# Stacked q and k loaded in two halves of groups, and the first maxima begun with the even groups

## The chip, the cores and the metric

One core of a Trainium2 chip runs the whole program. The metric is the device time of one execution in microseconds, median of several. Engines named below: PE is TensorE, DVE is VectorE, ACT is ScalarE, POOL is GpSimd, SP is SyncE, which here only issues transfers.

## The reference, cut to what matters

The kernel computes one transformer layer for 32 sequences of 256 tokens of width 128 in float32.

```python
Q, K, V = (split_heads(x @ W.T + b) for W, b in ((Wq, bq), (Wk, bk), (Wv, bv)))  # 16 heads of 8
scores = Q @ K.T / sqrt(8)                     # 256 x 256 for each head
scores = where(j > i, -inf, scores) - (i - j)  # causal, with a linear decay
x = layernorm(x + softmax(scores) @ V @ Wo.T + bo)
h = silu((x @ w1.T) * s1) * ((x @ w2.T) * s2)  # 128 -> 512
h = gelu((h @ h1.T) * sh1); h = gelu((h @ h2.T) * sh2)
x = layernorm(x + (h @ w3.T) * s3)
```

## The kernel before

The 32 sequences are worked in 16 **pairs** of two sequences, 512 tokens each. The 16 heads of a pair lie in 8 **groups** g of two heads, one head on partitions 0 to 63, the other on 64 to 127.

**Projection** (`project`, L314). x is transposed on PE (pxT), copied by DVE (xT), multiplied with wq_sb and wk_sb (pq, pk). `halves` (L295) splits each product in two parts that matmuls take without loss: ACT writes the high part (qhi, khi), DVE the rest (qlo, klo). Partition p*64 + d*8 + g of these tiles holds element d of head p of group g; the order comes from the way in which ACT copies the loaded weights to wq_sb and wk_sb (L165).

**Stacks** (`stack`, L305). For the scores, each group needs its own matrix with the elements of the head under each other: rows for the high and the low parts, mixed with constant rows for mask and decay that `fill` (L185) writes once into the buffers qs and ks (two each, used by pairs in turn). `stack` brings the parts there by transfers within the on-chip memory: four for q, four for k, of 0.25 MB each, all 8 groups in each. The first two pairs are stacked by SP (q) and ACT (k), pair 2 likewise at the end of step 0, all later ones by SP alone.

Every engine works through its instructions in the order in which they are written here; ACT's transfers stand among its arithmetic. Each transfer of SP and ACT takes one of eight completion semaphores in turn, and in the compiled order waits until the last transfer on that semaphore has landed.

**Maxima** (`row_maxima`, L373). A pair has 12 tiles of scores, numbered 3a, 3a+1, 3a+2 for a = 0 to 3: tile 3a holds the later half of the tokens of group 2a, tile 3a+1 that of group 2a+1, tile 3a+2 the earlier half of both groups. Each is eight or four matmuls and four mask matmuls on PE (s), and one DVE reduction (m) over 128x1024 numbers. Three buffers (ps_s) hold such tiles. `maxima_to_rows` (L407) transposes the maxima (pm), splits them (mhi on ACT, mlo on DVE) and brings them into qs by small transfers.

**Weighing** (`weigh`, L430) computes the scores again, now with the maxima as a row, takes exp on ACT (e) and masks on POOL. `outputs` (L470) multiplies with the values (pa), copies the result on ACT (oT), turns it back (pt) and divides (rec, on); `finish` (L512) multiplies with Wo (pon, onT, po) and adds x. The values of a pair come from `project_values` (L339): pv on PE, vaug on DVE.

**Order.** The start (L684 to L720) is written out by hand: project, fill and stack pairs 0 and 1, values of pair 0, maxima of pair 0 (tiles 0 to 5), values of pair 1, rows of groups 0 to 3, loads of the layer weights, tiles 6 to 11, rows of groups 4 to 7, two tiles of pair 1. Then `step(n)` (L725) weighs pair n, takes the maxima of pair n+1, projects and stacks pair n+2, and runs the feed-forward part (`feed`) of pair n-1. Step 0 has no feed-forward part; it checks the layer weights instead. In step 0 the stack of pair 2 is issued after the last weighing and before the last oT.

```python
    stack(1, "q", sp)
    stack(1, "k", act)
    project_values(0)
...
    for i in range(6):
        row_maxima(0, i)
    project_values(1)
    maxima_to_rows(0, (0,))
    loaded = load_layers(once)
    for i in range(6, 3 * G):
        row_maxima(0, i)
```

Of the kernel before, what the change touches and what calls it, by code (L numbers as in the profile page):

```python
# [8 lines left out]
F32 = mybir.dt.float32  # L9
# [3 lines left out]
AF = mybir.ActivationFunctionType  # L13
ALU = mybir.AluOpType
# [5 lines left out]
H, HD = 16, 8  # L20
# [9 lines left out]
W = 8  # L30
PAIRING, ROWS1, ROWS2 = 2, 62, 64


G, C = 4, 4
# [27 lines left out]
def tile_attn_ffn(  # L62
# [24 lines left out]
    pe, vec, act, sp = (InOrder(tc, e) for e in (nc.tensor, nc.vector, nc.scalar, nc.sync))  # L87
# [44 lines left out]
    nothing = const.tile([P, 1], F32, name="nothing")  # L132


    wq_sb = const.tile([P, D], F32, name="wq_sb")
    wk_sb = const.tile([P, D], F32, name="wk_sb")
    bq_sb = const.tile([P, 1], F32, name="bq_sb")
    bk_sb = const.tile([P, 1], F32, name="bk_sb")
# [4 lines left out]

    tri_q = const.tile([P, P], BF16, name="tri_q")
    raws = []
    for src, w_bias, bias, nm, eng in (
        (wqT, bq_sb, bq, "q", act), (wkT, bk_sb, bk, "k", sp),
    ):
        raw = setup.tile([P, D], F32, name=f"raw{nm}")
        eng.dma_start(out=raw, in_=src)  # L150
        raws.append(raw)
        for p in range(2):

            eng.dma_start(
                out=w_bias[64 * p : 64 * p + 64, :],
                in_=bias.rearrange("(f p) d e -> p d e f", p=2)[p],
            )

    def prepare(func):

# [2 lines left out]
    prepare(AF.Identity)  # L163
    act.dma_start(out=wv_sb, in_=wvT)
    for raw, dst, scale in zip(raws, (wq_sb, wk_sb), (HD**-0.5, 1.0)):  # L165
        act.activation(
            dst.rearrange("i (p d g) -> i p d g", p=2, g=W),
            raw.rearrange("i (g p d) -> i p d g", p=2, g=W), AF.Copy, scale=scale,
        )
    act.activation(bq_sb, bq_sb, AF.Copy, scale=HD**-0.5)  # L170
    act.dma_start(out=bv_sb, in_=bv.to_broadcast([P, D]))
    act.dma_start(out=bo_sb, in_=bo.to_broadcast([P, D]))

# [4 lines left out]
    def constants(nm, col):  # L178
        t = setup.tile([P, TOK], F32, name=f"{nm}const")
        vec.tensor_scalar(t, number, col["lo"], col["value"], ALU.is_ge, ALU.mult)  # L180
        vec.scalar_tensor_tensor(t, number, col["hi"], t, ALU.is_le, ALU.mult)
        vec.scalar_tensor_tensor(t, number, col["slope"], t, ALU.mult, ALU.add)
        fills[nm] = t, col["base"]

    def fill(dst, nm, eng, groups=slice(0, W)):  # L185
        t, base = fills[nm]
        to = dst[:, groups, :]
        t = t.unsqueeze(1).to_broadcast([P, groups.stop - groups.start, TOK])
        if eng is act:
            act.activation(to, t, AF.Identity, bias=base)  # L190
        else:
            eng.tensor_scalar(to, t, base, None, ALU.add)

    def column(nm):
        return setup.tile([P, 1], F32, name=f"col_{nm}")

    q, k = (
        {w: column(f"{nm}_{w}") for w in ("lo", "hi", "value", "slope", "base")} for nm in "qk"
    )
# [3 lines left out]
    for col, at in ((k, 64), (q, 0)):  # L203
# [6 lines left out]
    k["slope"] = q["base"]  # L210
    constants("k", k)
    fill(ks[0], "k", act)

    make_identity(nc, ident_b)
    nc.gpsimd.memset(tri_q, 0.0)
# [2 lines left out]
        out=tri_q, in_=tri_q, pattern=[[-1, P]], base=0, channel_multiplier=1,  # L218
# [30 lines left out]
    def load_layers(pool):  # L249
        got = {}  # L250
        for nm, src, k, o in layers:
            got[nm] = pool.tile([P, k, o], F32, name=f"{nm}_sb")
            sp.dma_start(out=got[nm], in_=src.rearrange("(k p) o -> p k o", p=P))
        return got
# [31 lines left out]
    def work(nm):  # L286
        return ps_w.tile([P, 512], F32, name=nm, tag="work")

    def two(nm):
        return ps_s.tile([P, 2, 512], F32, name=nm, tag="s")  # L290

    pairs = {}


    def halves(n, ps, bias, nm):  # L295
        pool = setup if n == 1 else hlp
        hi = pool.tile([P, TOK], F32R, name=f"{nm}hi_{n}", tag=f"{nm}hi")
        act.activation(hi, ps, AF.Identity, bias=bias)
        lo = pool.tile([P, TOK], F32R, name=f"{nm}lo_{n}", tag=f"{nm}lo")
        vec.scalar_tensor_tensor(  # L300
            lo, ps, bias, hi.bitcast(F32), ALU.add, ALU.subtract
        )
        return hi, lo

    def stack(n, nm, eng=sp):  # L305
        for r, part in {
            "q": ((0, 0), (1, 0), (2, 1), (3, 1)), "k": ((0, 0), (2, 0), (1, 1), (3, 1))
        }[nm]:
            eng.dma_start(
                out=pairs[n][nm][PAIRING + r :: W, :, :].bitcast(F32),  # L310
                in_=pairs[n][nm + "s"][part].bitcast(F32),
            )

    def project(n):  # L314
        xn = xs[n]
# [23 lines left out]
    def project_values(n):  # L339
        xT, v = pairs[n]["xT"], vaug[n % 2]  # L340
        pairs[n]["v"] = v
        pv = work(f"pv_{n}")
        for t in range(NT):
            pe.matmul(
                pv[:, t * D : (t + 1) * D], lhsT=xT[:, t * P : (t + 1) * P], rhs=wv_sb,
                start=True, stop=True,
            )
        to = v[:, :, 0 : H // 2 * VSLOT].rearrange("p t (r c k) -> p t r c k", r=2, c=C)
        src = pv.rearrange("p (t r e c d) -> p t r e c d", t=NT, r=2, e=2, c=C)
        bias = bv_sb.rearrange("p (r e c d) -> p r e c d", r=2, e=2, c=C)  # L350
        for r in range(2):
            for e in range(2):
                vec.tensor_tensor(
                    to[:, :, r, :, 2 * e * VHEAD : 2 * e * VHEAD + HD], src[:, :, r, e],
                    bias[:, r, e].unsqueeze(1).to_broadcast([P, NT, C, HD]), ALU.add,
                )
# [3 lines left out]
    def mask(blocks):  # L360


        for p, f in ((0, 0), (1, 1), (0, 1), (1, 0)):
            s, first, count = blocks(p)
            rows = slice(64 * p, 64 * p + 64)
            pe.matmul(
                s[64 * f : 64 * f + 64, :, first + 64 * f : first + 64 * f + 64],
                lhsT=ident_b[rows, rows],
                rhs=tri_q[rows, rows].unsqueeze(1).to_broadcast([64, count, 64]),
                start=False, stop=True, tile_position=(64 * p, 64 * f),  # L370
            )

    def row_maxima(n, i):  # L373

        q, k, m = (pairs[n][w] for w in "qkm")
        mv = m.rearrange("i b c (e p g) -> i e p g b c", e=2, p=2)[:, i // 6]
        a, part = divmod(i, 3)
        if part < 2:
            g = 2 * a + part
            s = two(f"s1_{n}_{g}").rearrange("i p (b j) -> i p b j", b=2)  # L380
            for b in range(2):
                for p in range(2):
                    rows = slice(64 * p, 64 * p + ROWS1)
                    pe.matmul(
                        s[:, p, b, :], lhsT=q[rows, g, b * T + P : (b + 1) * T],
                        rhs=k[rows, g, b * T : (b + 1) * T], start=(b == 0), stop=False,
                    )
            mask(lambda p: (s[:, p], P, 2))
            vec.tensor_reduce(mv[:, :, g % C, :, 1], s, AX.X, ALU.max, negate=True)
            return  # L390
        s = two(f"s1_{n}_{a}d").rearrange("i p (h b j) -> i p h b j", h=2, b=2)
        for h in range(2):
            for b in range(2):
                for p in range(2):
                    rows = slice(64 * p, 64 * p + ROWS1)
                    i0 = b * T
                    pe.matmul(
                        s[:, p, h, b, :], lhsT=q[rows, 2 * a + h, i0 : i0 + P],
                        rhs=k[rows, 2 * a + h, i0 : i0 + P],
                        start=(h == 0 and b == 0), stop=False,  # L400
                    )
        mask(lambda p: (s[:, p].rearrange("i h b j -> i (h b) j"), 0, 4))
        vec.tensor_reduce(
            mv[:, :, 2 * a % C : 2 * a % C + 2, :, 0], s, AX.X, ALU.max, negate=True
        )
# [273 lines left out]
    def run(gen):  # L679
        for _ in gen:  # L680
            pass
# [5 lines left out]
    fill(qs[0], "q", vec)  # L687
    run(ahead)
    stack(0, "q", sp)
    stack(0, "k", act)  # L690
    fill(ks[1], "k", act)
    ahead = project(1)
    next(ahead)
    fill(qs[1], "q", vec)
    run(ahead)
    stack(1, "q", sp)
    stack(1, "k", act)
    project_values(0)
    for a in range(G):
        act.dma_start(  # L700
            out=wo_sb[C * HD * a : C * HD * (a + 1), :],
            in_=woT[:, :, a, :].rearrange("c d o -> (c d) o"),
# [4 lines left out]
    yp = enter(tc.tile_pool(name="yp", bufs=2))  # L707
    lctx = ctx.enter_context(ExitStack())
    once = lctx.enter_context(tc.tile_pool(name="once", bufs=1))
    for i in range(6):  # L710
        row_maxima(0, i)
    project_values(1)
    maxima_to_rows(0, (0,))
    loaded = load_layers(once)
    for i in range(6, 3 * G):
        row_maxima(0, i)
    maxima_to_rows(0, (1,))
    load_scales()
# [165 lines left out]
```

## Time and profile before

| what | value |
|---|---|
| median of 3 runs | 822.67 us (822.67 to 824.28) |
| the profiled execution | 824.84 us |
| its span, first to last instruction | 822.9 us |
| mean granted clock of PE | 0.968 |
| PE busy in the span | 781.9 us (95%) |
| DVE busy | 635.9 us (77%) |
| ACT busy | 527.7 us (64%) |
| POOL busy | 260.6 us (32%) |
| stack transfers | 116 of 0.25 MB |

The page shows averages over the whole span. The start is short and differs from the rest, so it is read from the timeline. A line of the timeline has the start in us from the span's start, the length in us, the engine, the line (L58 is the helper that records most operations), the operation, the tile written and the tiles read, the shape, and how many instructions are merged; in brackets stands how long the engine had been idle before and who ended that. A q behind an engine's name marks its queue: an issue of a transfer, not work of the engine. Stretches give the busy time of each engine in a window, the clock that PE was granted (1.00 is full) and what the DMA engines moved.

### The profile page before, as it was taken

The numbers are of one execution on the slowest core, as the hardware profiler recorded it, in microseconds if no ns is written. First come the engines' busy times: TensorE is split into PE (matmuls) and PEld (weight loads), VectorE is DVE, ScalarE is ACT, GpSimd is POOL, SyncE is SP. The second block draws the span as 40 slices with busy tenths as digits, with TensorE's granted clock in tenths as the row PEclk, the third lists the DMA queues.
The fourth block names the chain that finished last, engine by engine and source line by source line (L and its number), as shares of the span: only waits on it lengthen the run. The fifth ranks groups of instructions, "written<-read, shape, count | busy, mean of one in ns | idle before, by whom it ended". The sixth has DMA issues, their size and how long they took to land.

```text
span 822.9 us, 17420 instructions
## 1 busy us (share of the span) xinstructions
PE 781.9 (95%) x7046; PEld 554.9 (67%) x7046; DVE 635.9 (77%) x1247; ACT 527.7 (64%) x719; POOL 260.6 (32%) x341
## 2 busy tenths in 40 slices
PE   4897999999999999999999999999999999999995
PEld 1664576676767677676767767676766767666673
DVE  6786777878788887888878887888888788873674
ACT  5055556667676776666576676657666676758673
POOL 5032413323142332414242341424233232424211
PEclk8569999999999999999999999999999999999997
DMA  6824040402304040320404041140404023000001
GB/s 148 209 63 108 14 106 14 105 16 60 73 14 106 27 107 14 81 53 14 106 27 106 14 104 29 36 97 15 107 26 104 4 57 64 14 5 14 0 3 41
DMA packets 39898, 47.49 MB, mean 58 GB/s; under 512 B 3968, under 2 KB 21632, under 8 KB 39808
## 3 DMA queue, kind: packets, MB, share of 16 engines
q1 hardware_dynamic: 37152, 42.82, 21.8%
q10 hardware_dynamic: 2656, 3.48, 1.9%
q8 instruction: 57, 0.93, 0.5%
q14 instruction: 33, 0.27, 0.1%
HBM read 7.48 MB, written 4.19 MB: 14 GB/s over the span
## 4 chain that ended last, share of the span: by engine, by line
PE 80%; ACT 5%; DVE 3%; issue 1%; DMA 1%; SPq 0%; POOL 0%; ACTq 0%; POOLq 0%; DVEq 0%
PE peven L58 14%; PE podd L58 14%; PE pa L58 11%; PE pw L58 10%; PE s L58 10%; PE s_2d L58 2%; PE s_3d L58 2%; PE s_1d L58 2%; PE po L58 2%; ACT e L58 2%; PE pt L58 2%; PE pk L58 2%; PE pv L58 2%; PE s_0d L58 1%; PE pq L58 1%; ACT yT L58 1%
## 5 line engine op out<-in xcount | busy, mean ns | idle before, releaser
L58 DVE TENSOR_REDUCE m<-s 128x4 f32<-128x1024 f32 x128 | 155.6, 1218 | 11.0 <-PE s L58 9.4
L58 ACT ACTIVATE e<-s 128x1024 f32<-128x1024 f32 x128 | 130.6, 1021 | 44.9 <-PE s L58 30.6
L463 POOL TENSOR_SCALAR_AFFINE_SELECT e<-e 128x512 f32<-128x512 f32 x128 | 83.1, 650 | 221.5 <-ACT e L58 192.2
L58 PE MATMUL podd<-h,h_near 128*128 128x512 f32 x512 | 131.4, 403 | 0.9 <-DVE m L58 0.5
L58 PE MATMUL peven<-hodd,h_near 128*128 128x512 f32 x512 | 122.7, 396 | 0.0
L58 PEld LDWEIGHTS peven<-hodd,h_near 128*128 128x128 f32 x512 | 95.7, 187 | 23.4 <-DVE hodd L58 0.3
L58 PEld LDWEIGHTS podd<-h,h_near 128*128 128x128 f32 x512 | 91.7, 188 | 23.1 <-DVE h L58 3.5
L58 ACT ACTIVATE hodd<-podd,sh 128x512 fp32r<-128x512 f32 x64 | 44.1, 688 | 62.8 <-PE podd L58 62.6
L58 PE MATMUL pw<-x1T,w_near 128*128 128x512 f32 x256 | 75.6, 418 | 1.1 <-DVE h0w L58 1.1
L58 PEld LDWEIGHTS s<-qs,ks 64*128 64x128 f32 x512 | 39.1, 189 | 51.9 <-DVE m L58 17.9
L58 PE MATMUL pa<-e,vaug 128*32 128x256 f32 x1024 | 72.2, 397 | 0.0
L274 POOL TENSOR_TENSOR rsa<-rsa,half 128x4 f32<-128x4 f32 x16 | 16.3, 1018 | 175.9 <-DVE rsa L58 175.9
L58 DVE SCALAR_TENSOR_TENSOR h0w<-pw,s,sg 128x512 f32<-128x512 f32 x64 | 47.9, 748 | 30.3 <-ACT sg L58 30.3
L58 PE MATMUL s<-qs,ks 64*128 64x256 f32 x512 | 65.6, 336 | 1.0 <-ACT e L58 0.5
L58 DVE TENSOR_TENSOR heven<-evenw,heven 128x512 fp32r<-128x512 f32 x64 | 44.2, 692 | 26.6 <-ACT evenw L58 26.1
L58 ACT ACT_TABLE_LOAD x47 | 60.3, 1283 | 3.5 <-issue 2.6
L58 ACT ACTIVATE sg<-pw,s 128x512 f32<-128x512 f32 x64 | 43.7, 684 | 28.2 <-PE pw L58 27.8
L58 ACT ACTIVATE heven<-peven,sh 128x512 fp32r<-128x512 f32 x48 | 33.4, 696 | 39.8 <-PE peven L58 39.8
L58 PE MATMUL s<-ks,qs 62*128 62x256 f32 x512 | 55.8, 297 | 2.6 <-ACT e_0d L58 2.1
L58 PEld LDWEIGHTS pw<-x1T,w_near 128*128 128x128 f32 x256 | 43.4, 188 | 18.4 <-ACT nothing L58 5.8
L581 POOL TENSOR_TENSOR h<-h0w,h 128x512 fp32r<-128x512 f32 x31 | 40.0, 1291 | 43.5 <-DVE h L58 41.2
L58 DVE TENSOR_TENSOR hodd<-oddw,hodd 128x512 fp32r<-128x512 f32 x64 | 43.7, 684 | 10.0 <-ACT oddw L58 9.8
(147 smaller groups left out, 1415.7 us busy)
## 6 DMA issues: line engine op xcount, KB each, us to landing
qs<-qhi SPq DMA_DIRECT2D x32, 256.0 KB
qs<-qlo SPq DMA_DIRECT2D x32, 256.0 KB
ks<-khi SPq DMA_DIRECT2D x26, 256.0 KB
ks<-klo SPq DMA_DIRECT2D x26, 256.0 KB
x<-in_x_dram SPq DMA_DIRECT2D x16, 256.0 KB
out_dram<-z SPq DMA_DIRECT2D x15, 256.0 KB
ks<-khi ACTq DMA_DIRECT2D x6, 256.0 KB
ks<-klo ACTq DMA_DIRECT2D x6, 256.0 KB
```

The source lines that it names most:

```text
L58: return lambda *args, **kw: self.tc.keep_in_program_order(call(*args, **kw))
L274: nc.gpsimd.tensor_tensor(rs, rs, half[:, 0:NT], ALU.pow)
L463: nc.gpsimd.affine_select(out=on_diagonal, in_=on_diagonal, pattern=[[0, on_diagonal.shape[1]], [1, P]], base=0, channel_multiplier=-1, co ...
L581: (nc.gpsimd if o < (1 if final else 2) else vec).tensor_tensor(h[:, 1, o, :], whole, h[:, 0, o, :].bitcast(F32), ALU.subtract)
```

## The change

Four things are changed.

- The columns of wq_sb and wk_sb are reordered so that the even groups lie on partitions 0 to 63 of the projected tiles and the odd groups on 64 to 127. ACT copies each weight in two instructions instead of one. The biases then are one run of memory each: SP loads both with one transfer each, where ACT and SP had issued two each. The scaling of bq_sb moves behind the first fill of ks.
- `stack` issues eight transfers of half the size instead of four: first the four for the even groups, then the four for the odd groups. This holds for all 16 pairs.
- For pair 1 alone, the DVE instructions that write qlo and klo are put off (`due`) until two maxima of pair 0 have been taken (`run_due`).
- The tiles of pair 0 are taken in the order 0, 3 (before the stack of pair 1), then 6, 9, 1, 2, 4, 5, then the values of pairs 0 and 1 and the rows of the first half, then 7, 8, 10, 11.

```diff
+    for w_bias, bias in ((bq_sb, bq), (bk_sb, bk)):
+        sp.dma_start(out=w_bias, in_=bias.rearrange("c d (e o) -> (c d e) o", o=1))
...
-        act.activation(
-            dst.rearrange("i (p d g) -> i p d g", p=2, g=W),
-            raw.rearrange("i (g p d) -> i p d g", p=2, g=W), AF.Copy, scale=scale,
-        )
-    act.activation(bq_sb, bq_sb, AF.Copy, scale=HD**-0.5)
+        for f in range(2):
+            act.activation(
+                dst[:, 64 * f : 64 * f + 64].rearrange("i (p d e) -> i p d e", p=2, e=C),
+                raw.rearrange("i (e f p d) -> i f p d e", f=2, p=2, e=C)[:, f], AF.Copy,
+                scale=scale,
+            )
...
     fill(ks[0], "k", act)
+    act.activation(bq_sb, bq_sb, AF.Copy, scale=HD**-0.5)
...
-        vec.scalar_tensor_tensor(
-            lo, ps, bias, hi.bitcast(F32), ALU.add, ALU.subtract
+        due.append(
+            lambda: vec.scalar_tensor_tensor(lo, ps, bias, hi.bitcast(F32), ALU.add, ALU.subtract)
         )
+        if n != 1:
+            run_due()
         return hi, lo
...
+        for f in range(2):
+            for r, part in {
+                "q": ((0, 0), (1, 0), (2, 1), (3, 1)), "k": ((0, 0), (2, 0), (1, 1), (3, 1))
+            }[nm]:
+                eng.dma_start(
+                    out=pairs[n][nm][PAIRING + r :: W, f::2, :].bitcast(F32),
+                    in_=pairs[n][nm + "s"][part][64 * f : 64 * f + 64, :].bitcast(F32),
+                )
...
     run(ahead)
+    for i in (0, 3):
+        row_maxima(0, i)
+    run_due()
     stack(1, "q", sp)
     stack(1, "k", act)
-    project_values(0)
...
-    for i in range(6):
+    for i in (6, 9, 1, 2, 4, 5):
         row_maxima(0, i)
+    project_values(0)
     project_values(1)
...
-    for i in range(6, 3 * G):
+    for i in (7, 8, 10, 11):
         row_maxima(0, i)
```

More of the change, by code (lines that the diff above doesn't have):

```diff
@@ L145, in tile_attn_ffn @@
     raws = []
-    for src, w_bias, bias, nm, eng in (
-        (wqT, bq_sb, bq, "q", act), (wkT, bk_sb, bk, "k", sp),
-    ):
+    for src, nm, eng in ((wqT, "q", act), (wkT, "k", sp)):
         raw = setup.tile([P, D], F32, name=f"raw{nm}")
@@ L151, in tile_attn_ffn @@
         raws.append(raw)
[L152 to L156, printed above, removed]
-            )
+    for w_bias, bias in ((bq_sb, bq), (bk_sb, bk)):
+        sp.dma_start(out=w_bias, in_=bias.rearrange("c d (e o) -> (c d e) o", o=1))
     def prepare(func):
@@ L165, in tile_attn_ffn @@
     for raw, dst, scale in zip(raws, (wq_sb, wk_sb), (HD**-0.5, 1.0)):
-        act.activation(
-            dst.rearrange("i (p d g) -> i p d g", p=2, g=W),
-            raw.rearrange("i (g p d) -> i p d g", p=2, g=W), AF.Copy, scale=scale,
-        )
-    act.activation(bq_sb, bq_sb, AF.Copy, scale=HD**-0.5)
+        for f in range(2):
[4 more added lines that the diff above has]
+            )
     act.dma_start(out=bv_sb, in_=bv.to_broadcast([P, D]))
@@ L299, in halves, with run_due @@
         lo = pool.tile([P, TOK], F32R, name=f"{nm}lo_{n}", tag=f"{nm}lo")
-        vec.scalar_tensor_tensor(
-            lo, ps, bias, hi.bitcast(F32), ALU.add, ALU.subtract
-        )
+        due.append(
+            lambda: vec.scalar_tensor_tensor(lo, ps, bias, hi.bitcast(F32), ALU.add, ALU.subtract)
+        )
+        if n != 1:
+            run_due()
         return hi, lo
+    due = []
+    def run_due():
+        while due:
+            due.pop(0)()
     def stack(n, nm, eng=sp):
[L306 to L312, printed above, removed]
+        for f in range(2):
[6 more added lines that the diff above has]
+                )
     def project(n):
```

## The prediction

> **What bounds the kernel now.** I read the busy table first: PE is busy 781.9 of 822.9 us, and the slices stay at 9 from the third slice on. The waits of PE from 200 to 600 us hold 2.0 us in all, so in the fourteen steady steps only PE work counts. What can move is the start. I then read the timeline there.
>
> ```profile
> 10.39 1.24 SPq L58 DMA_DIRECT2D qs<-qhi  x2
> 10.57 1.39 ACTq L58 DMA_DIRECT2D ks<-khi  x2
> 11.73 2.53 SPq L58 DMA_DIRECT2D qs<-qlo  x2
> 12.05 2.88 ACTq L58 DMA_DIRECT2D ks<-klo  x2
> 14.33 1.71 PE L58 MATMUL pk<-xT,wk_sb 128*128 128x512 f32 x2
> 14.98 3.71 ACT L58 ACTIVATE ks<-kconst,col_k_base 128x4096 fp32r<-128x4096 f32 x1 [4.44 <-DVE qs L58]
> 18.60 0.67 ACT L58 ACTIVATE qhi<-pq,bq_sb 128x512 fp32r<-128x512 f32 x1
> 19.30 0.75 DVE L58 SCALAR_TENSOR_TENSOR qlo<-pq,bq_sb,qhi 128x512 fp32r<-128x512 f32 x1 [4.46 <-ACT qhi L58]
> 19.97 0.74 DVE L58 SCALAR_TENSOR_TENSOR klo<-pk,bk_sb,khi 128x512 fp32r<-128x512 f32 x1
> 20.10 2.08 PE L58 MATMUL pv<-wv_sb,xT 128*128 128x128 f32 x8 [4.07 <-DVE qlo L58]
> 22.11 0.79 PE L58 MATMUL s<-ks,qs 62*128 62x256 f32 x4
> 23.21 1.23 DVE L58 TENSOR_REDUCE m<-s 128x4 f32<-128x1024 f32 x1
> ...
> 39.93 1.02 PE L58 MATMUL pm<-ident,m 128*8 128x128 f32 x4 [1.92 <-DVE m L58]
> 42.84 0.80 PE L58 MATMUL s<-qs,ks 64*128 64x256 f32 x4
> ```
>
> Start and length stand first. From 14.83 to 19.30 DVE has nothing to do, from 16.04 to 20.10 PE has nothing; then DVE works through twelve maxima almost without a break until 39.87, and the first weighing starts 3.0 us later. So DVE sets the end of this stage, and whatever starts its maxima earlier can gain.
>
> The second place is the end of step 0. Here ACT issues the k stack of pair 2, and the copy oT stands behind those issues in ACT's order.
>
> ```profile
> 69.78 1.43 ACTq L58 DMA_DIRECT2D ks<-khi  x2
> 71.31 2.44 ACTq L58 DMA_DIRECT2D ks<-klo  x2
> 72.42 1.07 PE L58 MATMUL pa<-e_3d,vaug 128*32 128x128 f32 x16
> 73.84 0.59 ACT L58 COPY oT<-pa 128x512 f32<-128x512 f32 x1 [3.06 <-PE pa L58]
> 77.61 1.16 PE L58 MATMUL po<-wo_sb,onT 128*128 128x128 f32 x8 [0.78 <-DVE onT L58]
> 79.09 0.73 PE L58 MATMUL s<-qs,ks 64*128 64x256 f32 x8 [0.33 <-DMA qs<-qhi]
> ```
>
> pa ends at 73.49 and ACT's last issue at 73.75: today they meet. From oT on everything is serial (oT, pt, rec, on, pon, onT, po, weighing of pair 1), so an ACT that is free later moves 79.09 by the same amount.
>
> **Start, 0 to 16 us.** The bias loads leave ACT's queue (2 issues, 1.30 us for the pair), one each goes to SP, where it takes the place of two; the weight copies become four of half size, bq's scaling (0.20) moves behind the first fill. All this lies beside DVE's fill of qs, which ends at 10.30 and holds qlo. I cost it at nothing; without that cover it is the 0.20 of bq.
>
> **The first maxima.** The even halves are the first eight transfers. The stretches of 1 us show 68, 274, 244, 219 and 336 GB/s from 11 to 16, so 1.05 MB has moved at about 15.7. By the semaphore counts of the trace the first transfer of this stack lands at 13.79, the fourth (1 MB) at 17.59, the eighth at 21.30. I put the even halves at 16.6, between 15.7 and 17.6. pk ends at 16.04, so the first s starts at 16.6 and its maximum, 1.10 later as now, at 17.7 instead of 23.21; two maxima of 1.18 end at 20.1.
>
> **A wait that is added.** In the program's order every transfer waits until the one eight places earlier has landed, since the completion semaphores are eight. Now eight stack transfers fit; sixteen do not. ACT's last k issue therefore waits for the even halves (16.6) and takes 0.6, so ACT is free at 17.2, not at 14.93. Behind it stand the fill of ks (3.71), qhi and khi of pair 1, and for qhi wait qlo, klo and, in DVE's order, ten maxima. Now qlo comes 4.32 after the fill starts (14.98 to 19.30), so it comes at 21.6; DVE idles 1.5 from 20.1. klo ends 1.41 later, at 23.0; three maxima (3.55) end at 26.55.
>
> **The values.** Both pv now follow tile 5 of pair 0. Its matmuls can start when the third of those three maxima frees their buffer, at 26.55: 1.5 for that tile, 2.08 and 2.07 for the two pv at half clock, pm 1.06, mhi and mlo with their handovers 1.3 (31.76 to 33.02 now), then four maxima 4.72: together 12.7, end 39.3. Before, pv of pair 0 lay in DVE's wait for the first s. At full clock (pv 1.06 each, rows of 70 to 80 us) the same chain ends about 1.5 earlier, 37.8: then DVE's own maxima and not PE carry part of it. I take the middle, 38.6, a gain of 1.3 against 39.87. Bounds: ACT not held at all (qlo at 20.1, full clock) gives 36.3, a gain of 3.6; even halves at 17.6 and half clock give 40.3, a loss of 0.4.
>
> The clock row: from 20 to 30 PE is busy 9.90 of 10.00 us, with a granted clock of 0.50. The Trainium skill ("TensorE: Matmul & The Clock Gate", part 1) says that one busy window of about 3.4 us lifts the half clock, with a free phase; in this trace ten busy us did not, so the trace decides. By the rule alone the two pv would lift the clock within themselves and the chain would end near 38.
>
> What follows the maxima is unchanged and covered: the stack of pair 1 is read only after 39, the weights w1 to w3 (issued 33.73 to 36.16) go out about 1.5 later and are first copied at 44.64 to 49.40.
>
> **End of step 0.** ACT has eight issues instead of four. The first four at about 0.6 each run from 69.78 to 72.2. The fifth waits for the first to land: a 0.25 MB transfer took 3.40 (10.39 to 13.79 above), half of it some 0.5 less at 245 GB/s, so 72.7. The last waits for the fourth (71.6 + 2.9 = 74.5) and ends at 75.1. oT then starts at 75.2 instead of 73.84: **1.4 lost**, and nothing covers it. Lower bound: eight issues of 0.54 without a wait, 74.1, a loss of 0.3. Upper bound: every landing takes the full 3.4 plus 0.6 beside SP's q stack, 76.3, a loss of 2.5; a PE that idles longer here may also fall to 0.50 for one stretch, as at 71 us, another 0.8.
>
> **Steady steps.** SP issues 16 transfers instead of 8. In one step:
>
> ```profile
> 204.55 1.43 SPq L58 DMA_DIRECT2D ks<-klo  x2
> 208.69 0.56 SPq L58 DMA_DIRECT2D qs<-mhi  x1
> 211.43 0.56 SPq L58 DMA_DIRECT2D qs<-mlo  x1
> ```
>
> The stack begins at 200.54; 16 issues of 0.60 end at 210.2, past mhi (1.5 late) and before mlo, which waits for DVE. The rows are read at 225.20, so 12 us of PE work in the feed-forward part hide it. Without that cover it would be 1.5 a step, 21 us in all. The added semaphore waits of PE, ACT and DVE (51, 17 and 21 ns each) stand in queues that are ahead. I take nothing.
>
> On splitting, the Trainium skill ("DMA: Bandwidth & Descriptors", "Rules for kernel authors") speaks against this change: two transfers to disjoint halves share the same engines and serialize, so it advises one transfer. The trace agrees on the sum (DMA share 0.99 or more from 12 to 31 us). By the rule the odd half lands no sooner than 21.3; the change needs the even half alone.
>
> **Sum.** -1.3 at the maxima, +1.4 at oT, 0 elsewhere: +0.1 us. The profiled execution took 824.84 (span 822.9 and 1.9 around it); the median of the three runs is 822.67, and I set the sum on it: 822.8. The half clock from 36.2 to 56.7 in step 0 can begin and end one stretch of 3.4 us earlier or later: at most 1.7 either way, not counted in the middle. A measurement here can tell about 0.2%, 1.65 us, from no change.
>
> **Rivals.**
> - *Faster.* The maxima gain near their bound: full clock for the values, ACT held for less. For it: DVE has 4.5 idle us ahead of 19.30 and 1.56 at 22; against it: the ACT chain to qhi. Gain 3.2, oT costs 0.8: 820.3. Chance 0.29.
> - *Slower.* ACT, standing on landings with fill and oT behind it, is one mechanism in both places. With the even halves at 17.6 the maxima lose 0.4, and oT costs 2.5: 825.6. It decides as soon as ACT's standing at oT costs over 1.65 more than the maxima gave. For it: single issues took up to 2.14 in the loaded stretch from 12 to 24 us, both queues are loaded at 72 us; against it: halves carry half the bytes. Chance 0.30.
> - *It doesn't do what it says.* Even and odd halves interleave, so the even ones land only at 20: two maxima end at 23.5, qlo comes at 25.0, 3.4 later than above; that turns the gain of 1.3 into a loss of 2.1, and with 1.4 at oT it is 826.2. The rings take transfers in order in the landings above (13.79 to 21.30), so it gets 0.04.
>
> **How the numbers follow.** Near tie, 0.37: 821.0 to 824.3, 822.8 itself. The range of 820.3 to 825.3 leaves out the far half of the slower cases and the last of the faster. Chances: faster 0.29, within 0.2% 0.37, slower 0.34 (0.30 and 0.04).
>
> **What would show it.** The first m at 17.7 and qlo of pair 1 at 21.6 with an idle DVE ahead of it; fill of ks at 17.2; pm of the second half near 38.6; oT 1.4 later against its pa than now; steady steps of the same length. An oT that starts at once after pa, or a fill at 15, would prove my wait wrong and give the faster case; a longer steady step would prove my cover wrong.

## The result, and the profile after

The changed kernel is slower: 829.9 us median of 6 runs (826.55 to 832.08) against 823.45 of the kernel before (822.67 to 824.28, 6 runs), ratio 1.0072 with a 95% interval of 1.0058 to 1.0087. The forecast was 822.8, in a range of 820.3 to 825.3. The profiled execution after took 830.99 us (span 829.1, mean granted clock 0.963), 6.15 more than that of before (824.84, span 822.9, clock 0.968).

The first view is again the timeline of the start, now of the changed kernel, with the columns as before (start, length, engine, operation, shapes, idle time ahead and who ended it).

```profile
10.65 1.25 ACTq L58 DMA_DIRECT2D ks<-khi  x2
13.60 2.44 ACTq L58 DMA_DIRECT2D ks<-khi  x2
16.08 1.74 ACTq L58 DMA_DIRECT2D ks<-klo  x2
17.87 3.71 ACT L58 ACTIVATE ks<-kconst,col_k_base 128x4096 fp32r<-128x4096 f32 x1 [7.25 <-DMA ks<-khi]
18.35 0.51 PE L58 MATMUL s<-ks,qs 62*128 62x256 f32 x4 [1.95 <-DMA qs<-qhi]
21.49 0.67 ACT L58 ACTIVATE qhi<-pq,bq_sb 128x512 fp32r<-128x512 f32 x1
22.19 0.75 DVE L58 SCALAR_TENSOR_TENSOR qlo<-pq,bq_sb,qhi 128x512 fp32r<-128x512 f32 x1 [0.74 <-ACT qhi L58]
28.57 3.78 PE L58 MATMUL pv<-wv_sb,xT 128*128 128x128 f32 x16
39.99 1.01 PE L58 MATMUL pm<-ident,m 128*8 128x128 f32 x4 [1.92 <-DVE m L58]
44.86 1.12 PE L58 MATMUL s_0d<-ks,qs 62*128 62x128 f32 x8 [1.16 <-ACT e L58]
```

The even halves do their part: the first tile of scores starts at 18.35 in place of 22.11. But the fill of ks now stands behind the last k issue and starts 2.89 later (17.87 against 14.98), qlo of pair 1 with it (22.19 against 19.30), and the second pm comes at 39.99 where it came at 39.93. Nearly four microseconds of head start are gone by then. The last row is the first thing in step 0 that the sum does not have: before, this tile of pair 1 started at 43.46, ahead of the first exp (43.72), in this row:

```profile
43.46 1.12 PE L58 MATMUL s_0d<-ks,qs 62*128 62x128 f32 x8
```

Now it waits 1.16 for that exp.

The same view at the end of step 0:

```profile
70.83 1.02 ACT L58 ACTIVATE e_3d<-s_3d 128x1024 f32<-128x1024 f32 x1
70.85 1.42 ACTq L58 DMA_DIRECT2D ks<-khi  x2
72.37 1.58 ACTq L58 DMA_DIRECT2D ks<-klo  x2
73.99 2.71 ACTq L58 DMA_DIRECT2D ks<-khi  x2
76.74 1.54 ACTq L58 DMA_DIRECT2D ks<-klo  x2
78.38 0.59 ACT L58 COPY oT<-pa 128x512 f32<-128x512 f32 x1 [6.53 <-DMA ks<-khi]
79.01 1.11 PE L58 MATMUL pt<-ident,oT 128*128 128x128 f32 x4 [5.31 <-ACT oT L58]
82.73 0.69 DVE L58 COPY onT<-pon 128x512 f32<-128x512 f32 x1
85.48 1.22 PE L58 MATMUL s<-qs,ks 64*128 64x256 f32 x8
```

ACT's eight issues run for 7.43 us, from 70.85 to 78.28; before, four took 3.97. pa had ended at 73.71, so PE stands idle for 5.31, and the granted clock falls to a half in the same stretch (experiment 3 asks whether the one causes the other). In the table by stretches, now of the changed kernel (us, busy time of PE, PEld, DVE, ACT and POOL with the number of instructions, granted clock, DMA share, GB/s):

```profile
74.00:78.00 4.00, 0.00 (x0) 0.00 (x0) 0.00 (x0) 0.00 (x0) 0.00 (x0) 0.95 0.77 199
78.00:82.00 4.00, 2.99 (x14) 2.99 (x15) 0.97 (x4) 0.59 (x1) 0.00 (x0) 0.50 1.00 252
86.00:90.00 4.00, 3.75 (x32) 2.59 (x28) 2.75 (x12) 3.62 (x4) 2.14 (x3) 0.50 0.00 0
90.00:94.00 4.00, 4.00 (x28) 2.36 (x24) 3.61 (x5) 0.20 (x2) 3.16 (x7) 0.50 0.22 65
```

and of the kernel before, with its row of onT:

```profile
78.00:82.00 4.00, 2.40 (x27) 1.89 (x26) 2.01 (x10) 2.31 (x3) 0.92 (x1) 1.00 0.73 151
76.87 0.69 DVE L58 COPY onT<-pon 128x512 f32<-128x512 f32 x1
```

The chain behind oT (pt, pv, pon, po) runs at half clock: from oT to onT it takes 4.35 in place of 3.03. In the records the half clock lasts from 77.6 to 94.7. Before, the same place had two stretches of 3.4 (70.3 to 73.7 and 84.0 to 87.4).

From here on the steps are equal: from the load of x for pair 6 to that of pair 15 it is 426.1 us in both, and PE is busy 398.02 of the 400 us from 200 to 600 in both. The whole difference is made in the first 90 us:

| mark | before | after | later by |
|---|---|---|---|
| second pm | 39.93 | 39.99 | 0.06 |
| e_3d, end of step 0's exps | 69.76 | 70.83 | 1.07 |
| oT | 73.84 | 78.38 | 4.54 |
| onT | 76.87 | 82.73 | 5.86 |
| first exp of pair 1 | 79.69 | 86.38 | 6.69 |
| last store issued | 817.88 | 824.75 | 6.87 |

So about 0.1 comes from the start, 1.0 from step 0, 3.5 at oT, and 2.3 behind oT up to the last store, most of it between oT and the first exp of pair 1, at half clock. The span grew by 6.2 and not by 6.87, since the last store's issue itself took 0.97 before and 0.38 after.

### The profile page after: what moved, and what is told of

It reads as the page before. It is cut to its first block, busy times and chain, and to the rows that moved or that the text cites. A ratio compares the mean times of both kernels' runs of the same rounds, so it can differ in the third digit from the quotient of the medians.

```text
span 829.1 us, 17631 instructions
## 1 busy us (share of the span) xinstructions
PE 785.4 (95%) x7046; PEld 557.9 (67%) x7046; DVE 635.9 (77%) x1247; ACT 528.1 (64%) x721; POOL 260.8 (31%) x341
## 4 chain that ended last, share of the span: by engine, by line
PE 80%; ACT 5%; DVE 4%; issue 1%; DMA 0%; POOL 0%; ACTq 0%; DVEq 0%; POOLq 0%
PE peven L58 14%; PE podd L58 13%; PE pa L58 11%; PE s L58 10%; PE pw L58 10%; PE po L58 2%; PE s_2d L58 2%; PE s_3d L58 2%; PE s_1d L58 2%; PE pt L58 2%; ACT e L58 2%; PE pv L58 2%; PE pk L58 2%; PE s_0d L58 1%; PE pq L58 1%; ACT yT L58 1%
## 5 line engine op out<-in xcount | busy, mean ns | idle before, releaser
L58 ACT ACTIVATE heven<-peven,sh 128x512 fp32r<-128x512 f32 x48 | 33.4, 696 | 39.8 <-PE peven L58 39.8
```

What stands on the lines that cost most here:

```text
L58: return lambda *args, **kw: self.tc.keep_in_program_order(call(*args, **kw))
```

## The experiments

**Theory A**: ACT issues transfers, and stands on each until an earlier one on the same completion semaphore has landed; what follows in its order (the fill of ks, oT) is late, and PE, idle meanwhile, is put on half clock. In step 0 the compiled order gives ACT's k transfers four of the eight semaphores in turn (the first transfers of SP's q stack have the others), so its fifth k transfer may go out only when its first has landed. **Theory B**: the loss is in the smaller transfers themselves, or in the new order of columns and maxima. All times below stand against runs of the kernel before in the same job.

**1. The k stack of pair 2 on SP.** Two kernels with the same line changed, one from the kernel after, one from the kernel before:

```diff
-            stack(n + 2, "k", sp if n else act)
+            stack(n + 2, "k", sp)
```

> The changed kernel, with the k stack of pair 2 issued by SP behind the q stack, so that ACT issues nothing ahead of oT in step 0. Theory A (ACT stands on landings in front of oT, 4.5 us later than before, and PE then runs at half clock for longer): oT starts within 0.2 us of the end of pa, the half clock behind 77 us is shorter, and the time falls from 829.9 to between 824 and 825.5; what stays over the kernel before is the about 1 us by which step 0 runs later. Theory B (the loss comes from the half-size transfers themselves or from the new order of columns and maxima, and oT only looks late): 828.5 to 830.

> The kernel before with the same one edit, as a control. Theory A: oT moves by 0.25 us at most, since pa ends at 73.49 and ACT's last issue at 73.75, so 823.0 to 824.0, no difference that can be measured. If instead SP's eight issues in a row make the stack of pair 2 land too late for its maxima in step 1, it is 825 or more, and e1 would carry that cost too. Theory B: 823.0 to 824.0 too.

Measured: from after, 825.8 us (824.14 to 827.55), ratio 1.0025 (1.0015 to 1.0035); from before, 825.62 (823.78 to 827.77), ratio 1.0028 (1.0018 to 1.0038), where before has 823.6. With ACT free, oT starts at 73.27, 0.1 behind the end of pa. The control was to cost nothing, unless SP's issues made the stack late, and it costs 2: SP issues q and k one after the other, and PE then waits for the stack. In the timeline of the first:

```profile
83.50 0.80 PE L58 MATMUL s<-ks,qs 62*128 62x256 f32 x4 [3.18 <-DMA ks<-klo]
```

In the control this wait is 3.59. So the edit moves the wait elsewhere, but on top of it the rest of the change costs nothing that can be measured (825.8 against 825.62). That speaks for ACT's issues of this one stack as the main cost; it does not settle it, since a wait for the stack can hide a lateness that lies ahead of it.

**2. The kernel before, pair 2's stacks alone in halves.** The halves are of the tokens here, which needs no new order of columns; `SPLIT = (2,)`.

```diff
+        for t in (slice(0, T), slice(T, TOK)) if n in SPLIT else (slice(0, TOK),):
...
-                out=pairs[n][nm][PAIRING + r :: W, :, :].bitcast(F32),
-                in_=pairs[n][nm + "s"][part].bitcast(F32),
+                    out=pairs[n][nm][PAIRING + r :: W, :, t].bitcast(F32),
+                    in_=pairs[n][nm + "s"][part][:, t].bitcast(F32),
```

> The kernel before with one part of the change: the stacks of pair 2 alone go out in two halves, here halves of the tokens of each sequence pair (rows of 1 KB instead of 2 KB), the columns and the order of the start as before. Theory A: ACT's eight issues take 7 us instead of 3.9, oT comes 3 to 4 us later, PE idles over 4 us and falls to half clock: 827 to 829.5. Theory B: 823 to 824.5, oT within 1 us of where it was.

Measured: 827.68 us (826.29 to 829.56), ratio 1.0052 (1.0035 to 1.0068), 4.1 over before. Its timeline has the row of after, with pa done at 71.66:

```profile
76.56 0.58 ACT L59 COPY oT<-pa 128x512 f32<-128x512 f32 x1 [6.75 <-DMA ks<-khi]
```

Nothing else of the change is in this kernel, so the loss at oT needs neither its columns nor its order of maxima.

**3. PE fed while ACT stands.** The kernel after with four extra matmuls, whose result nobody reads, between pa and pt in step 0.

```diff
+                if n == 0 and u == 2:
+                    fed = work("fed")
+                    for _ in range(4):
+                        pe.matmul(fed, lhsT=wv_sb, rhs=pairs[n + 2]["xT"], start=True, stop=True)
```

> The changed kernel with four added matmuls of 128x512 on PE between pa and pt at the end of step 0, whose output nothing reads: PE has work while ACT stands on its issues. Theory A in its second part (the idle PE is given half clock, which then costs some 2 us in pv, po and the first tiles of step 1): the granted clock stays at 1.00 from 77 to 95 us, and the time is 827.5 to 828.5 in spite of the added work. If the half clock there follows something else than PE's idling: clock as in the changed kernel, and 829.5 to 831.

Measured: 828.26 us (826.83 to 829.0), ratio 1.0055 (1.0041 to 1.0069). oT stays late at 78.19, but the stretches behind it are at full clock:

```profile
77.00:82.00 5.00, 2.43 (x18) 1.82 (x17) 2.33 (x8) 0.59 (x1) 0.00 (x0) 1.00 1.03 251
```

In the changed kernel the same stretch reads:

```profile
77.00:82.00 5.00, 2.99 (x14) 2.99 (x15) 0.97 (x4) 0.59 (x1) 0.00 (x0) 0.56 0.91 229
```

The lengths of the instructions agree (po takes 1.16 in place of 2.08). From oT to onT it is 3.02 in place of 4.35, from oT to the first exp of pair 1 it is 5.46 in place of 8.00. So the idle PE is what the half clock followed here, and the half clock is 1.3 of the loss at onT and 2.5 at that exp; of this the times show 1.4 (by the ratios) to 1.6 (by the medians).

**4. The odd half behind oT.** The kernel after; in step 0 ACT issues the odd halves of pair 2's k stack after oT.

```diff
-            stack(n + 2, "k", sp if n else act)
+            stack(n + 2, "k", sp if n else act, (0, 1) if n else (0,))
...
-            for _ in range(3):
+            for u in range(3):
                 next(side)
+                if n == 0 and u == 1:
+                    stack(2, "k", act, (1,))
```

> The kernel after, only that ACT issues the odd halves of the k stack of pair 2 behind oT instead of ahead of it; number and size of the transfers stay. Theory A: oT starts within 0.5 us of the end of pa (73.7 to 74.9 in place of 78.38), PE's idle time ahead of pt falls from 5.3 to about 1, the half clock from 77.6 to 94.7 is gone or short as in the kernel before, and the time is 824 to 825.5 where after has 829.9; what stays above before (823.5) is about 1 us from step 0. Theory B (the half-size transfers themselves, wherever they are issued): 828.5 to 830.

Measured: 824.26 us (823.27 to 825.4), ratio 1.0018 (1.0009 to 1.0027), where before has 822.92. pa ends at 72.83, and:

```profile
72.98 0.58 ACT L58 COPY oT<-pa 128x512 f32<-128x512 f32 x1 [2.54 <-DMA ks<-khi]
```

The same transfers of the same size are issued, only elsewhere, and about three quarters of the loss is gone (ratio 1.0072 to 1.0018). Theory B falls for this place, and it is the issues that stand ahead of oT on ACT that cost the time.

**5. The kernel before, pair 0's stacks alone in halves** (`SPLIT = (0,)` in the edit of experiment 2).

> The kernel before, only with the four stacks of pair 0 split in two halves of the tokens, so sixteen transfers of 0.125 MB in place of eight of 0.25 MB; order of columns, of the maxima and every other transfer stay. Theory A (ACT stands on landings ahead of the fill of ks, and the fill holds back qhi, qlo and so the maxima of pair 0): the fill of ks starts at 17.5 to 18.5 us in place of 14.98, qlo of pair 1 at about 22 in place of 19.30, pv of pair 0 with it, the first s near 22.3 as before, pm of the second half 1 to 2.5 later than 39.93; time about 824.5 to 826 where before has 823.5. Theory B (the order of columns and maxima costs the time, a split start does not): the fill may be late, pm of the second half stays within 0.4 of 39.93, time 823.5.

Measured: 827.55 us (826.34 to 828.16), ratio 1.0053 (1.0039 to 1.0067), 4.6 over before and more than expected. Its timeline:

```profile
17.66 3.71 ACT L59 ACTIVATE ks<-kconst,col_k_base 128x4096 fp32r<-128x4096 f32 x1 [7.12 <-DMA ks<-klo]
22.79 2.08 PE L59 MATMUL pv<-wv_sb,xT 128*128 128x128 f32 x8 [6.13 <-DVE qlo L59]
24.79 0.79 PE L59 MATMUL s<-ks,qs 62*128 62x256 f32 x4
42.61 1.01 PE L59 MATMUL pm<-ident,m 128*8 128x128 f32 x4 [1.92 <-DVE m L59]
```

Fill and qlo are as late as in after (17.66, 21.98). In the old order pv of pair 0 waits for qlo and the maxima behind pv, so the second pm is 2.68 late (I had expected the first tile at 22.3; I had overlooked that pv stands ahead of it). So splitting costs the start 2.7, and the new order of tiles wins 2.6 of it back (42.61 to 39.99). That is where the gain went: it pays for the fill that the split itself has put back. Of the 4.6 in the medians the profiles show 2.8; the profiled execution of before lies 1.4 to 1.9 above its medians, which is most of the rest. The Trainium skill ("DMA: Bandwidth & Descriptors", "Rules for kernel authors") advises one transfer in place of two to disjoint partition halves, because the two serialize. The halves are of the tokens here and in experiment 2; both runs lose, as that advice would have it, but what they lose stands in ACT's queue, and they do not test its reason.

**What holds ACT, by the landings.** Theory A says that ACT stands on landings. The semaphore counts of the traces show when each transfer landed, and they bear this out at the start and only in part at oT. In the run above, ACT's last four issues for pair 0 start at 13.64, 14.81, 15.98 and 17.08, each 0.02 behind the landing of the transfer four places earlier in ACT's order. At the end of step 0 in the changed kernel, one issue of the eight does so: the last starts at 77.74, the fourth transfer landed at 77.72. The fifth did not wait, for the first transfer had landed at 73.53, while ACT was still in its fourth issue (to 73.95). The waits there come to 0.4 of the 7.43 us; nearly all the rest is the length of the issues themselves, up to 1.99 for the sixth:

```profile
74.72 1.99 ACTq L58 DMA_DIRECT2D ks<-khi  x1
76.74 0.61 ACTq L58 DMA_DIRECT2D ks<-klo  x1
77.74 0.54 ACTq L58 DMA_DIRECT2D ks<-klo  x1
```

An issue of SP, begun at 75.02, ended at 76.71, together with that sixth one. Why both took so long is open.

**6. Pair 0's odd halves behind the fill.** The kernel after:

```diff
-    stack(0, "k", act)
+    stack(0, "k", act, (0,))
     fill(ks[1], "k", act)
...
     run(ahead)
+    stack(0, "k", act, (1,))
     for i in (0, 3):
```

> The kernel after, only that ACT issues the odd halves of the k stack of pair 0 behind the fill of ks, qhi and khi of pair 1 instead of ahead of the fill; the end of step 0 stays as in after, with its loss there. Theory A: the fill of ks starts at 14.9 to 15.2 in place of 17.87, qhi of pair 1 at about 18.6 in place of 21.49, qlo at 19.3 to 20.3 in place of 22.19; the odd halves of k land later, near 24 to 25, and hold tiles 1 and 2. pm of the second half comes at 38 to 39.5 in place of 39.99, time 828.5 to 829.9 where after has 829.9. If PE at half clock, and not ACT, sets the end of the maxima, pm of the second half stays within 0.3 of 39.99 and the time does not move.

Measured: 830.72 us, but only 4 runs (827.35 to 831.65), ratio 1.0099 (1.0084 to 1.0114): no gain in the time. In its profile (the execution of 827.35) the fill starts at 13.44 and qhi at 17.05, 4.4 earlier than in after; qlo comes only at 20.60, behind two maxima in DVE's order, and PE then waits for the odd halves of k, which are issued later (the bracket names a transfer of q; by the semaphore counts the last odd transfer of k for pair 0 landed at 23.99):

```profile
24.18 0.80 PE L58 MATMUL s<-ks,qs 62*128 62x256 f32 x4 [3.53 <-DMA qs<-qhi]
```

The second pm comes at 39.32, 0.67 earlier. So ACT freed, the landings themselves are next, close behind. Why the other three executions took over 830 is open; they have no trace.

**7. Both values behind pm.** The kernel after, with the values of pairs 0 and 1 computed behind the first pm, which gives s_0d of pair 1 a buffer freed by DVE again.

```diff
-    project_values(0)
-    project_values(1)
     maxima_to_rows(0, (0,))
     loaded = load_layers(once)
+    project_values(0)
+    project_values(1)
```

> The kernel after, only that the values of pairs 0 and 1 (pv and vaug) are computed behind the first pm instead of ahead of it. With this order the tile s_1_0d of pair 1 in step 0 gets a buffer that DVE frees, as in the kernel before, and not the one that the first exp of ACT frees. Theory: in after that wait for ACT (1.16 us) is what put the end of step 0 back by 1.07 (e_3d 70.83 against 69.76). So here s_1_0d of pair 1 starts at about 43.5 to 43.8 in place of 44.86, e_3d at 69.8 to 70.2, and the time is 0.7 to 1.2 below after: 828.7 to 829.3. Rival: the wait is regained before the end of step 0 and the lateness has another source; then e_3d stays at 70.8 and the time at 829.9. The pv move can also change pm of the second half by some tenths.

Measured: 832.94 us (831.91 to 833.53), ratio 1.0121 (1.0106 to 1.0137), a miss. The second pm comes at 44.72. One reason is ACT once more:

```profile
35.21 0.57 ACT L58 CAST mhi<-pm 8x512 fp32r<-8x512 f32 x1 [11.27 <-DMA wo_sb<-in_woT_dram]
36.55 2.07 PE L58 MATMUL pv<-wv_sb,xT 128*128 128x128 f32 x8 [2.17 <-DVE mlo L58]
```

pm was done at 32.67; mhi stood behind the pair's last k issues and four loads of wo until 35.21, and the second pv behind mlo, which cost PE 2.17. In the kernel after this stand is 0.9 (pm done at 33.21, mhi at 34.13). The larger part is the move itself: both pv, 4.0 together, now lie between pm and the next tile, while the first pm came only 0.5 earlier (31.65 against 32.15). Step 0 itself did become shorter: from the first exp to e_3d it takes 24.41, or 19.9 if its 9.1 us at half clock count half; in after it is 27.05, or 20.4. The wait for the exp thus costs step 0 about half a microsecond to one.

**8. Three versions from the theory.** First both moves, experiments 4 and 6 together:

> Both moves at once: the kernel after with the odd halves of the k stack of pair 0 behind the fill of ks, qhi and khi of pair 1, and the odd halves of the k stack of pair 2 behind oT. Theory A (ACT standing on landings in both places): pm of the second half near 39.3 as in the run with the first move alone, oT within 0.3 of the end of pa as in the run with the second alone, and the wait of s_1_0d for the first exp stays (about 0.9). Time 823.2 to 824.2, that is 0 to 1 below the run with the second move alone (824.3) and within 0.2% of before (823). Theory B: the first move's gain of 0.7 at pm is lost again in step 0, time 824.3 or more.

Measured: 823.06 us (821.44 to 825.11, 12 runs), ratio 0.9996 (0.9986 to 1.0006), level with before. oT starts 0.14 behind pa, the second pm at 39.07. Then, on top of it, the loads of wo and the values of pair 1 behind the first pm:

```diff
-    for a in range(G):
-        act.dma_start(out=wo_sb[C * HD * a : C * HD * (a + 1), :], in_=...)
...
     project_values(0)
-    project_values(1)
     maxima_to_rows(0, (0,))
+    for a in range(G):
+        act.dma_start(out=wo_sb[C * HD * a : C * HD * (a + 1), :], in_=...)
     loaded = load_layers(once)
+    project_values(1)
```

> The run with both moves, and also: the four loads of wo on ACT are issued behind the first mhi in place of ahead of it, and the values of pair 1 (pv, vaug) behind the first pm. With this order s_1_0d of pair 1 waits for DVE as in the kernel before, not for the first exp. Theory: the wait for the exp costs 0.9 us of step 0 (with it, step 0 from the first exp to e_3d takes 20.4 to 20.5 us when the time at half clock is counted half, without it 19.5 to 19.9), and mhi, no longer behind wo, starts when pm is done (33.2 to 33.5). Time 822.0 to 823.2, below before (823) by 0 to 1. Rival: the values of pair 1, behind pm, hold back the maxima that follow, as in the run with both values behind pm, where pm of the second half came at 44.72; then 824 or more.

Measured: 822.03 us (819.92 to 824.56, 12 runs) where before has 823.35, ratio 0.998 (0.9968 to 0.9993): the only version here that beats both kernels, by 0.2% (the interval reaches from 0.07% to 0.32%). Its timeline:

```profile
31.91 0.57 ACT L58 CAST mhi<-pm 8x512 fp32r<-8x512 f32 x1 [12.57 <-PE pm L58]
43.29 1.11 PE L58 MATMUL s_0d<-ks,qs 62*128 62x128 f32 x8
43.56 1.02 ACT L58 ACTIVATE e<-s 128x1024 f32<-128x1024 f32 x1 [2.17 <-PE s L58]
71.91 0.58 ACT L58 COPY oT<-pa 128x512 f32<-128x512 f32 x1 [1.98 <-PE pa L58]
```

mhi starts when pm is done, s_0d starts ahead of the exp, oT starts when pa is done. Step 0 takes 25.35, or 19.8 with the half clock counted half, against 20.5 in the version before it. The second pm is 0.7 later than there (39.77), so step 0 and what follows gave more than that; wo, the values and the buffer were moved together, and their shares are not told apart. From oT to the first exp of pair 1 it is 8.00 in the trace of the version before it, which has half clock there until 80.7, and 5.54 in this one, at full clock; whether the moves did that is not shown. Last, the values of pair 0 ahead of tiles 4 and 5:

> As the run before it, but the values of pair 0 stand ahead of the maxima of tiles 4 and 5, where PE waits for the odd halves of q and k, instead of behind them. If PE's wait there (24 us, 1.4 to 3.5 us long in the runs so far) can hold a pv of 2.08 us at half clock, pm of the second half comes 0.5 to 1.5 earlier than in the run before it and the time falls by as much: 821.0 to 822.7. If the pv only pushes the tiles behind it back, the time is that of the run before it, within 0.5.

Measured: 823.23 us (822.14 to 825.4), ratio 1.0001 (0.999 to 1.0012). The second pm comes at 40.77, 1.0 later: the pv pushes the tiles behind it back and fills no wait. Neither expectation holds; it costs 1.2.

## Why the prediction was wrong

- **What bounds the kernel, and the steady steps: right.** Only the first 90 us differ. SP's sixteen issues in a step end later than worked out, against mhi too (mhi is 2.7 late, not 1.5), and the rows are covered as said: 0 a step.
- **Start, nothing: nearly.** The first stack issues start 0.1 (ACT) to 0.3 (SP) later.
- **The first maxima: too early.** Even halves at 16.6; the first tile's wait ended at 18.35, the first maximum starts at 19.09 and not 17.7. The upper bound was 17.6. By the semaphore counts the last even half landed at 18.22. ACT's odd issues start at 13.60, beside SP's even ones, which end at 14.65.
- **The added wait: mechanism right, size short.** ACT's last issue starts at 17.08, 0.02 behind the landing of its fourth transfer. ACT free at 17.2, measured 17.8; qlo at 21.6, measured 22.19.
- **The values: gain of 1.3, measured a loss of 0.06**, within the bounds (3.6 gained to 0.4 lost). Of the 1.4 between forecast and trace, 0.6 is the later qlo and 0.7 the middle taken between two clocks: PE was at half clock until 33.4, and the chain worked out for half clock (39.3 with qlo at 21.6, so 17.7 behind it) came true, with the last maximum ending 17.75 behind qlo. That it fits so well is in part luck, since mhi stands 0.9 behind the loads of wo, which the sum does not have, and pv, pm and the maxima make this up.
- **Step 0, "what follows the maxima is unchanged": wrong.** The moved tiles and values gave s_0d another buffer and a wait of 1.16; e_3d is 1.0 later against the second pm. The compiled order names this wait (DVE before, ACT after), so it could have been read.
- **oT, 1.4 lost: the step that failed.** It lost 3.5 against e_3d, and with PE's clock behind it 4.8 at onT; the upper bound was 2.5. The last issue did wait for the fourth transfer, as said; the fifth did not wait for the first. What was sized wrongly is the way to that landing. I priced the first four issues at 0.6, from quiet rows, and the landing of the fourth at 2.9 behind its issue, and so had the last issue end 5.3 after the first began. The fourth issue began 2.4 after the first, in place of 1.8, its transfer landed 4.45 after that, and the last issue ended at 7.43. An earlier landing alone would have helped little: the seventh issue ended 0.37 ahead of it. The rows I had quoted from just this place were nearer: four issues took 1.43 and 2.44, with the gap 3.97. Twice that is 7.94, and oT 4.0 later. That this comes so close is partly luck, for the four hold a wait of 1.0 (the fourth issue, at 73.20, for the first transfer, which landed at 73.18) and the eight one of 0.4.
- **Half clock: left out of the middle, and it came.** I had counted it as a possible 0.8 beside the upper bound of oT; experiment 3 gives 1.4 to 1.6 in the times.
- **The rivals.** The case on the slower side named the place and, for the fill, the mechanism, ACT standing on landings with fill and oT behind it, and the point from which it decides (oT over 1.65 more than the maxima gave). Its price was 2.9 over before (825.6 against 822.67); it was 6.5 over 823.45, the median of before that the result has. The weight of 0.37 on a near tie rested on the price of 1.4.

## What to carry to other kernels

A transfer issue on an engine that also computes is an instruction in its queue: splitting a transfer in two puts twice the issues, and any waits on landings, in front of whatever stands behind. Price them by the rows of that very place under its own load, and ask what stands behind them; here the odd halves that nobody needed yet belonged behind the copy that everybody waited for. A gap on the critical path of several microseconds is paid twice where the matmul clock falls in it, and moving tiles can change which buffer, and so which engine, a later tile waits for.

## What the hardware showed that I had not expected

- **Issues get slow under load.** SP's stack issues run at about 0.62 us in the steady steps of both kernels; with both queues loaded four of ACT's (whole transfers) took 0.54 to 0.88 each, eight (half ones) 0.54 to 1.99, on average 0.70 and 0.84 without the waits between them. Half the bytes did not make an issue shorter. The Trainium skill ("DMA: Bandwidth & Descriptors", "Anatomy of one DMA — SWDGE (gpsimd) path") says that a wait on a semaphore happens on the issuing sequencer ahead of the dispatch. The issues that wait agree with that: they start 0.02 behind the landing (77.74 behind 77.72), and oT stands behind them on ACT.
- **The clock.** After 5.31 idle us PE was at 0.50 from 77.6. The Trainium skill ("TensorE: Matmul & The Clock Gate", Part 1) has a window of about 3.4 idle us drop the clock and one busy window lift it again. The drop agrees with the trace; the lift does not: from 90 to 94 PE was busy 4.00 of 4.00 us, from 86 to 90 3.75, all at 0.50, and full clock came at 94.7. Four matmuls in the idle gap (experiment 3) kept it at 1.00. In the records of both kernels up to 100 us the half clock comes in stretches of 3.41, 13.65, 17.07 and 20.48 us, whole multiples of 3.41.
